# A state-space phase on Trainium2: one activation table for Exp and Ln, decays made early around Silu, and softplus steps moved by a slot

## The chip, the cores and the metric

The kernel runs on one core of a Trainium2 chip. The metric is the device time of one execution in microseconds. The engines that matter are TensorE (PE, with its weight loads PEld), VectorE (DVE), ScalarE (ACT), GpSimd (POOL) and SyncE (SP, whose queue issues the DMAs named here). Each works through its instructions in program order and meets the others by semaphores.

## The reference, cut to what matters

The whole program is a block of four layers in float32 with residuals: a selective state-space layer (SSM) fed by `ctx_1024`, a mixture of experts, a cross-attention and a ternary feed-forward. The change lies in the SSM layer alone:

```python
x = einsum('ed,bld->bel', in_proj_w, ctx)            # 512 channels, 512 steps, 4 batches
u = silu(causal_depthwise_conv(x, conv_w) + conv_b)  # 4 taps
x_dbl = einsum('ke,bel->bkl', x_proj_w, u)           # dt_lo (16), Bm (16), Cm (16)
delta = softplus(dt_proj_w @ dt_lo + dt_proj_b)
A = -exp(A_log)                                      # 512 channels x 16 states
state = state * exp(delta * A) + (delta * u) * B_t   # for each step t
y_t = sum over the 16 states of state * C_t
y = (y + D * u) * silu(layernorm(x_in))
```

## The kernel before

Channels lie on the 128 partitions, so a batch has four chunks `c` of channels, and a chunk has 16 states, taken two at a time. One *slot* is a pair of states of one chunk: `seq` lists 4 batches x 4 chunks x 8 pairs = 128 slots, `q` counts them and `s = q % 32` is the slot within its batch. The recurrence over 512 steps is one scan instruction on DVE (line 511) for two states, 1024 elements long; the first column of `delta` is overwritten with a huge value, so that the second state starts anew.

For slot q these steps are needed:

- `inputs(q)`, line 488 on POOL: dBu = B x (delta u), made two slots ahead in a ring of 3.
- `decays(q)`, line 497 on ACT: two Exp into dA, made one slot ahead, in PSUM, a ring of 2.
- `scan(q)`, lines 511 and 512: the scan on DVE, then the product with C, on POOL for pairs 0, 2 and 4 and on DVE for the others. The result hc is in a ring of 3.
- `sums(q)`, line 517: PE turns hc and adds it up over the states in yT; it is issued at the end of slot q + 1.

Around them the main loop puts other work into the slots, in an order written out by hand. While batch b is scanned, `ahead(b + 1, s)` prepares the next batch: the convolution as products on PE in slots 0 to 15 (`conv`, line 304; its weights come by `load_wcv` from DRAM), Silu of u in slot 17 (`silu_u`), the projection in 18 and 19, and then, for each of the four chunks, softplus in two-slot steps. Softplus is max(p, 0) + ln(1 + exp(-|p|)) with a correction of the rounding of 1 + e: `steps_a` (the product pdt on PE, Abs, Exp and +1 on ACT), `steps_ln` (Ln on ACT), `steps_b` (lines 443, 444 and 446 on DVE, then du on POOL, line 448). `silu_gz` (slot 28) makes the gate's Silu; `gate`, `take_gate` and `result` apply it. `rows` loads B and C as rows broadcast to all partitions, 1 MB each.

Two more jobs ride along for the attention layer: `values` (every other slot, line 470; `take_values` copies pv and stores v), and `Keys` (`task`: a product pk; `evict`: Square and a scaled copy on ACT, and a store; `squares`: sums of squares on PE; `take`: their small eviction). `key_steps` is called twice a slot, with `ends` false near its start and true at its end.

PSUM is full: banks `pa` (pd, pdt, pgz and most of the keys), `pin` (the convolution, and ln for batches after the first), `pv`, `yT`, and two double banks for dA. ACT's functions live in table sets; a function outside the loaded set is preceded by ACT_TABLE_LOAD in the trace.

Of the kernel before, what the change touches and what calls it, by code (L numbers as in the profile page):

```python
# [17 lines left out]
F32 = mybir.dt.float32  # L18
# [11 lines left out]
P = 128  # L30
# [192 lines left out]
        return z  # L223


@with_exitstack
def ssm_phase(ctx, cm, x_all, w, kv, dr):

# [9 lines left out]
    pda = ctx.enter_context(tc.tile_pool(name="a_pda", bufs=2, space=PSUM))  # L238
    KC = CTX // P
    NP = DS // 2  # L240
    R = 64

    def load_x(b):
# [35 lines left out]
    dtT = cp.tile([DR + 1, DM], F32, name="dtT")  # L279
    nc.scalar.dma_start(dtT[0:DR, :], w["dt_proj_wT"])  # L280
    nc.scalar.dma_start(dtT[DR:, :], w["dt_proj_b"])
    nc.scalar.activation(negA, negA, AF.Exp)

    nc.vector.tensor_scalar(negA, negA, -1.0, -1e-27, ALU.mult, ALU.min)
# [52 lines left out]

    def silu_0(c):
        nc.scalar.activation(st[0]["u"][c], st[0]["u"][c], AF.Silu)

# [33 lines left out]
    def silu_u(b):  # L374
        for u in st[b]["u"]:
            nc.scalar.activation(u, u, AF.Silu)

    def stats(b, c):
        sts = small.tile([P, 6], F32, name="st_a")
        nc.vector.bn_stats(sts, x_all[:, b * NC + c, :])  # L380
        nc.vector.bn_aggr(st[b]["mv"][:, c, :], sts)

    def norm(b):
        s = st[b]
        ve = small.tile([P, NC], F32, name="ve_a")
        nc.gpsimd.tensor_scalar(ve, s["mv"][:, :, 1], EPS, None, ALU.add)
        s["rstd"] = small.tile([P, NC], F32, name="rstd_a")
        nc.gpsimd.tensor_tensor(s["rstd"], ve, half, ALU.pow)
        s["nmr"] = small.tile([P, NC], F32, name="nmr")
        nc.gpsimd.tensor_tensor(s["nmr"], s["mv"][:, :, 0], s["rstd"], ALU.mult)  # L390
        nc.gpsimd.tensor_scalar(s["nmr"], s["nmr"], -1.0, None, ALU.mult)

    def silu_gz(b):
        s = st[b]
        for c in range(NC):
            gz = pool[5].tile([P, S], F32, name="gz")
            nc.scalar.activation(gz, x_all[:, b * NC + c, :], AF.Silu, bias=s["nmr"][:, c:c + 1],
                                 scale=s["rstd"][:, c:c + 1])
            s["gz"].append(gz)

    def project(b):
        pd = st[b]["pd"] = ps.tile([R, S], F32, name="pd", tag="pa")
# [14 lines left out]
                t, bc_dram[b, row:row + NG, :].unsqueeze(0).to_broadcast([P, NG, S]))  # L417
            st[b][name].append(t)

    def steps_a(b, c):  # L420

        s = st[b]
        pdt = s["pdt"] = ps.tile([P, S], F32, name="pdt", tag="pa")
        nc.tensor.matmul(pdt, dtT[:, c * P:(c + 1) * P], s["xd"][0:DR + 1, :], start=True,
                         stop=True)
        e, wt = (pool[1].tile([P, S], F32, name=n) for n in ("e", "wt"))
        s["e"], s["wt"] = e, wt
        nc.scalar.activation(e, pdt, AF.Abs)
        nc.scalar.activation(e, e, AF.Exp, scale=-1.0)
        nc.scalar.activation(wt, e, AF.Identity, bias=cm.ones[:, 0:1])  # L430

    def steps_ln(b):

        s = st[b]
        s["ln"] = (pool[5].tile([P, S], F32, name="ln", tag="gz") if b == 0 else
                   ps.tile([P, S], F32, name="ln", tag="pin"))
        nc.scalar.activation(s["ln"], s["wt"], AF.Ln)

    def steps_b(b, c):

        s = st[b]
        e, wt, ln = s["e"], s["wt"], s["ln"]
        nc.vector.scalar_tensor_tensor(e, wt, 1.0, e, ALU.subtract, ALU.subtract)
        nc.vector.tensor_tensor(e, ln, e, ALU.subtract)
        delta = pool[5].tile([P, S], F32, name="delta")
        nc.vector.scalar_tensor_tensor(delta, s["pdt"], 0.0, e, ALU.max, ALU.add)
        du = pool[5].tile([P, S], F32, name="du")
        nc.gpsimd.tensor_tensor(du, delta, s["u"][c], ALU.mult)


        nc.gpsimd.memset(delta[:, 0:1], RESET)
        s["delta"].append(delta)
        s["du"].append(du)


# [32 lines left out]
            nc.gpsimd.tensor_tensor(dBus[q], st[b]["bb"][i // 2][:, j:j + 2, :],  # L488
                                    st[b]["du"][c].unsqueeze(1).to_broadcast([P, 2, S]), ALU.mult)

    def decays(q):
        if q < len(seq):
            b, c, i = seq[q]
            dAs[q] = pda.tile([P, 2, S], F32, name="dA")
            for j in range(2):
                n = 2 * i + j
                nc.scalar.activation(dAs[q][:, j, :], st[b]["delta"][c], AF.Exp,  # L497
                                     scale=negA[:, c, n:n + 1])
# [56 lines left out]
    def ahead(b, s):  # L555

        if s % 4 == 0 and 4 <= s <= 16:
            take_conv(b, s // 4 - 1)
        if s < 16:
            conv(b, s // 4, (s % 4 * 2, s % 4 * 2 + 1))  # L560
        if s in (4, 8):
            load_wcv(b, s // 4 + 1)
        if s == 17:
            silu_u(b)
            for c in range(NC):
                stats(b, c)
            norm(b)
        if s == 18:
            project(b)
        if s == 19:  # L570
            take_project(b)
        if s in (22, 24, 26, 28):
            steps_b(b, (s - 22) // 2)
        if s in (20, 22, 24, 26):
            steps_a(b, (s - 20) // 2)
        if s in (21, 23, 25, 27):
            steps_ln(b)
        if s == 28:
            silu_gz(b)
        if s == 20 and b + 1 < B:  # L580
            start(b + 1)
        if s == 20 and b + 1 == B:
            load_ctx(0, again=True)
        if s in (26, 28, 30, 31):
            rows(b, (26, 28, 30, 31).index(s))

    def key_bank(shape, name):
        return ps.tile(shape, F32, name=name, tag="pin" if name == "pk" and keys.wide else "pa")  # L590

    keys = Keys(cm, w, kv, small, lambda n: pool[1].tile([P, S], F32, name=f"k_{n}",
                                                         tag={"sq": "e", "kT": "wt"}[n]),
# [1 line left out]

    def key_steps(b, s, ends):

        if b > 0 and not ends and s == 0:
            keys.take()
        if b < B - 1:  # L600
            for j, at in enumerate((14, 17, 29) if b == 0 else (3, 6, 11, 14, 17, 29)):
                if not ends and s == at - 3:
                    keys.load(j, j + 1, pool[2], "k_w")
                if not ends and s == at + 3:
                    keys.take()
                if ends and s == at:
                    keys.wide = at > 16
                    keys.task(b + 1, j)
                if ends and s == at + 1:
                    keys.evict()  # L610
                if ends and s == at + 2:
                    keys.squares()
        if b == B - 2 and ends and s in (18, 22):
            h = s - 18
            keys.load(h, h + HG, pool[2], "wcvc")
        if b == B - 1:
            h = s // 2
            if not ends and s % 2:
                keys.take()

            if ends and s == 31:
                keys.squares()
            if ends and s % 2:
                keys.evict()
            if ends and s % 2 == 0:
                if s < 30:
                    keys.squares()
                keys.wide = True
                keys.task(0, h)
                if h in (HG, 2 * HG):  # L630
                    keys.load(h + HG, h + 2 * HG, pool[2], "wcvc")

    def start(b):
        load_ctx(b)
        load_wcv(b, 0)
        load_wcv(b, 1)


    fold(3)
# [25 lines left out]
    for c in range(NC):  # L665
        stats(0, c)
    norm(0)
    steps_a(0, 0)
    steps_ln(0)
    steps_b(0, 0)  # L670
    decays(0)
    inputs(0)
    inputs(1)
    load_wcv(1, 0)
# [1 line left out]
    load_wv(0)  # L676
    for g in range(1, DS // NG):
        rows(0, g)
    SL = NC * NP
    for q, (b, c, i) in enumerate(seq):  # L680
        inputs(q + 2)
        decays(q + 1)
        key_steps(b, q % SL, False)
        if i == 2 and q > 2:
            result(*seq[q - 3][:2])
        scan(q)
        if i == 3:
            direct(b, c)
        if q == 0:
            silu_gz(0)  # L690
        if q % SL == 8 and b + 1 < B:
            load_x(b + 1)
        if q in (4, 6, 13):
            steps_b(0, len(st[0]["du"]))
        if q in (2, 4, 11):
            steps_a(0, len(st[0]["du"]))
        if q in (3, 5, 12):
            steps_ln(0)
        late = 6 if c == NC - 1 or q < NP else 1
        if i == late + 1:  # L700
            take_gate(b, c)
        if b + 1 < B:
            ahead(b + 1, q % SL)
        if i == late:
            gate(b, c)
        if q % 8 == 2 and q + 8 < len(seq):
            load_wv(q // 2 + 4)
        if q % 2:
            values((b + 1) % B, q % SL // 2, wvs[q // 8])
        elif q > 0:  # L710
            take_values(*last)
        last = (b + 1) % B, q % SL // 2
        sums(q - 1)
        key_steps(b, q % SL, True)
    sums(len(seq) - 1)
    take_values(*last)
    keys.take()
    keys.squares()
    keys.take()
    result(B - 1, NC - 1)  # L720
# [1525 lines left out]
```

## Time and profile before

| | us |
|---|---|
| median of 3 runs (lowest, highest) | 2767.82 (2764.25, 2768.01) |
| the profiled execution | 2769.29 |
| its span, first to last instruction | 2767.4 |
| PE busy in the span | 2539.8 |
| DVE busy | 1486.8 |
| ACT busy | 1274.1 |
| POOL busy | 1181.3 |

The SSM phase is the first fifth: its first scan starts at 40.44 us and its last at 579.20 us, and the routing of the experts begins behind it. Its scans of slot 0 start at 40.44, 193.46, 334.44 and 476.75 us for the four batches; those of slot 16 at 115.05, 256.12, 396.77 and 529.33. A stretch of the profile from one of these to the next is half a batch, 16 slots. "Idle before" in a group is the time in which the engine stood in front of its instructions, with what ended it.

### The profile page before, as it was taken

To read this page: it belongs to the slowest core of one execution; us is meant where nothing else is said; L and a number is where in the kernel's file an instruction comes from. 1 tells how busy PE (TensorE), PEld (TensorE's weight loads), DVE (VectorE), ACT (ScalarE), POOL (GpSimd) and SP (SyncE) were. 2 spreads that over 40 slices of the span, in tenths; PEclk is the share of its full clock that TensorE was granted. 3 is DMA by queue.
4 is the path that set the end of the run, shared out by engine and by line. 5 is a ranking of instruction groups with operands and counts; after the bars stand their busy time and mean duration, and the time that the engine had idled before them with its cause. 6 is when DMAs were issued, how large, how long until landed. Compare 5 with 4: busy or idle time off the path is not lost. (4 is left out here: it accounts for less than half of the span.)

```text
span 2767.4 us, 29904 instructions
## 1 busy us (share of the span) xinstructions
PE 2539.8 (92%) x10107; PEld 1436.0 (52%) x10158; DVE 1486.8 (54%) x2546; ACT 1274.1 (46%) x2363; POOL 1181.3 (43%) x1121
## 2 busy tenths in 40 slices
PE   5989897986899999999985989999999999999997
PEld 2545454653456566666663544445555554555543
DVE  5887877966322223333443365545665666544445
ACT  6675757754323322222332443445555554555543
POOL 4888887961333334443433333224431443121212
PEclk8979797987999999999998999999999999999999
DMA  6253535322656656668986344323332443221200
GB/s 243 81 200 102 200 102 188 119 84 80 195 181 209 209 179 220 222 224 306 343 284 209 122 147 131 95 88 126 114 96 80 126 126 99 80 80 51 64 31 19
DMA packets 198352, 405.21 MB, mean 146 GB/s; under 512 B 30372, under 2 KB 71908, under 8 KB 193073
## 3 DMA queue, kind: packets, MB, share of 16 engines
q1 hardware_dynamic: 155566, 249.86, 26.8%
q0 software_dynamic: 40576, 153.19, 17.4%
q8 instruction: 83, 1.36, 0.2%
q14 instruction: 77, 0.62, 0.1%
q10 hardware_dynamic: 2050, 0.18, 0.1%
HBM read 321.22 MB, written 81.92 MB: 146 GB/s over the span
## 5 line engine op out<-in xcount | busy, mean ns | idle before, releaser
L1827 DVE TENSOR_REDUCE mx<-psc 128x1 f32<-128x512 f32 x256 | 176.5, 690 | 452.5 <-PE psc L1824 446.9
L1191 PE MATMUL pg<-xT,wg 128*128 128x284 f32 (+12 forms) x1536 | 399.9, 404 | 14.2 <-ACT h L1202 12.8
L1191 PEld LDWEIGHTS pg<-xT,wg 128*128 128x128 f32 x1536 | 282.6, 194 | 95.1 <-issue 29.7
L1830 ACT ACTIVATE e<-psc,mx 128x512 f32<-128x512 f32 x256 | 176.0, 687 | 320.4 <-DVE mx L1827 320.0
L488 POOL TENSOR_TENSOR dBu<-bb,du 128x1024 f32<-128x1024 f32 x128 | 299.9, 2367 | 26.8 <-DVE dA L511 19.8
L1132 POOL DMA_INDIRECT xg<-xn_dram,tok x168 | 180.7, 1076 | 209.9 <-PE pt L1175 164.7
L1824 PE MATMUL psc<-kT,qT 128*128 128x512 f32 x512 | 264.0, 597 | 1.6 <-ACT qT L1818 1.6
L1851 PE MATMUL po<-eT,v 128*128 128x512 f32 x512 | 235.0, 602 | 10.3 <-ACT eT L1845 10.2
L1790 PE MATMUL pq<-Wq,xnT 128*128 128x512 f32 x512 | 235.0, 603 | 0.7 <-ACT xnT L1749 0.7
L1860 PE MATMUL px<-Wo,oT 128*128 128x512 f32 x512 | 231.5, 595 | 0.0
L511 DVE TENSOR_TENSOR_SCAN dA<-dA,dBu 128x1024 f32<-128x1024 f32 x80 | 183.1, 2289 | 56.9 <-ACT dA L497 46.4
L1801 POOL TENSOR_SCALAR qms<-qms 128x4 f32<-128x4 f32 x64 | 25.5, 398 | 418.1 <-DVE qms L1799 417.2
L1844 PEld LDWEIGHTS pet<-ident,e 128*128 128x128 f32 x1024 | 126.2, 141 | 147.7 <-issue 124.6
L497 ACT ACTIVATE dA<-delta,negA 128x512 f32<-128x512 f32 x256 | 176.5, 692 | 19.0 <-DVE hc L512 12.6
L470 PE MATMUL pv<-Wv,ctxb 128*128 128x512 f32 x256 | 148.1, 709 | 28.7 <-ACT v L476 28.7
L517 PEld LDWEIGHTS yT<-ident,hc 128*128 128x128 f32 x1024 | 130.1, 153 | 83.1 <-issue 57.9
L1851 PEld LDWEIGHTS po<-eT,v 128*128 128x128 f32 x512 | 97.3, 192 | 139.0 <-issue 117.7
L1132 POOL DMA_INDIRECT yg<-y_dram,pos x128 | 128.9, 1007 | 87.5 <-SPq L757 38.5
L1236 DVE COPY yo<-po 128x512 f32<-128x512 f32 x68 | 47.0, 690 | 219.4 <-PE po L1225 219.3
L1844 PE MATMUL pet<-ident,e 128*128 128x128 f32 x1024 | 154.5, 274 | 6.4 <-DVE e L1836 6.4
L517 PE MATMUL yT<-ident,hc 128*128 128x128 f32 x1024 | 145.3, 293 | 11.1 <-POOL hc L512 6.4
L1836 DVE TENSOR_SCALAR e<-e,tot 128x512 f32<-128x512 f32 x256 | 150.5, 588 | 9.1
(352 smaller groups left out, 4384.6 us busy)
## 6 DMA issues: line engine op xcount, KB each, us to landing
y_dram<-yo SPq DMA_DIRECT2D x110, 256.0 KB
bb<-bc_dram SPq DMA_DIRECT2D x16, 1024.0 KB
cb<-bc_dram SPq DMA_DIRECT2D x16, 1024.0 KB
v_dram<-v SPq DMA_DIRECT2D x64, 256.0 KB
k_dram<-k_kT SPq DMA_DIRECT2D x64, 256.0 KB
Wq<-Wq SPq DMA_DIRECT2D x16, 1024.0 KB
kT<-k_dram SPq DMA_DIRECT2D x64, 256.0 KB
rk<-r_dram SPq DMA_DIRECT2D x64, 256.0 KB
```

The costliest lines, as they stand in the source:

```text
L488: nc.gpsimd.tensor_tensor(dBus[q], st[b]["bb"][i // 2][:, j:j + 2, :], st[b]["du"][c].unsqueeze(1).to_broadcast([P, 2, S]), ALU.mult)
L497: nc.scalar.activation(dAs[q][:, j, :], st[b]["delta"][c], AF.Exp, scale=negA[:, c, n:n + 1])
L511: nc.vector.tensor_tensor_scan(*flat, 0.0, ALU.mult, ALU.add)
L517: nc.tensor.matmul(yT[:, lc, :], t[:, lc * P:(lc + 1) * P], cm.ident, is_transpose=True, start=first and lc == 0, stop=last, skip_group_ch ...
L1132: nc.gpsimd.indirect_dma_start(out=t[0:n, :], out_offset=None, in_=table, in_offset=bass.IndirectOffsetOnAxis(ap=index, axis=0))
L1191: nc.tensor.matmul(pg[:, 0:n], s["wg"][:, c, m * P:(m + 1) * P], s["xT"][:, c, 0:n], start=c == 0, stop=c == NC - 1)
L1790: nc.tensor.matmul(pq.rearrange("p h d -> p (h d)"), xnTs[b * NC + i][:, c, :], s["Wq"][:, c, :], start=c == 0, stop=c == NC - 1)
L1824: nc.tensor.matmul(pscore, st[b, g]["qT"][:, h, i * P:(i + 1) * P], ks[n], start=True, stop=True)
L1827: nc.vector.tensor_reduce(mx, pscore, AX.X, ALU.max, negate=True)
L1844: nc.tensor.transpose(pt[:, kc, :], e[:, kc * P:(kc + 1) * P], cm.ident)
L1851: nc.tensor.matmul(po, v[:, kc, :], eT[:, kc, :], start=kc == 0, stop=kc == KB - 1)
L1860: nc.tensor.matmul(px, oTs[j * HG + h][:, i * P:(i + 1) * P], st[b, g]["Wo"][:, h, :], start=h == 0, stop=h == HG - 1)
```

## The change

- `tables` asks for one table set that holds Exp and Ln. It is called before the first Exp and after each group of Silu.
- In slots 16 and 28 the decays of the slot after next are made as well, into an SBUF buffer of the tag `wcvc` instead of PSUM (`early=True`). The two loads of convolution weights that used this tag from slot 20 go to the ends of slots 29 and 31.
- `silu_gz` goes from slot 28 to 29; the layernorm's statistics go from slot 17 to slots 12 to 15, and `norm` to 16.
- The product pdt is a step of its own, `dt`, issued ahead of the slot's values and sums (for chunk 0 at the end of slot 19). A Relu on ACT reads pdt as well and writes the tile that becomes delta, so `steps_b` adds two SBUF tiles and does not read pdt. +1 moves from `steps_a` to `steps_ln`.
- `steps_b` goes from the middle of slots 22, 24, 26, 28 to the end of 21, 23, 25, 27; `step_du` (du on POOL) stays in 22, 24, 26, 28.
- The keys' tasks start a slot earlier, their evictions and takes move within the slots, and their banks are chosen by task.

```diff
+def tables(nc):
+    nc.scalar.preload_act_table_set("natural_log_exp_and_others")
...
     nc.scalar.dma_start(dtT[DR:, :], w["dt_proj_b"])
+    tables(nc)
     nc.scalar.activation(negA, negA, AF.Exp)
...
     def silu_0(c):
         nc.scalar.activation(st[0]["u"][c], st[0]["u"][c], AF.Silu)
+        if c == NC - 1:
+            tables(nc)
...
         for u in st[b]["u"]:
             nc.scalar.activation(u, u, AF.Silu)
+        tables(nc)
...
             s["gz"].append(gz)
+        tables(nc)
...
-    def steps_a(b, c):
+    def dt(b, c):
+        pdt = st[b]["pdt"] = ps.tile([P, S], F32, name="pdt", tag="pa")
+        nc.tensor.matmul(pdt, dtT[:, c * P:(c + 1) * P], st[b]["xd"][0:DR + 1, :], start=True,
+                         stop=True)
+    def steps_a(b):
         s = st[b]
-        pdt = s["pdt"] = ps.tile([P, S], F32, name="pdt", tag="pa")
-        nc.tensor.matmul(pdt, dtT[:, c * P:(c + 1) * P], s["xd"][0:DR + 1, :], start=True,
-                         stop=True)
-        e, wt = (pool[1].tile([P, S], F32, name=n) for n in ("e", "wt"))
-        s["e"], s["wt"] = e, wt
-        nc.scalar.activation(e, pdt, AF.Abs)
-        nc.scalar.activation(e, e, AF.Exp, scale=-1.0)
-        nc.scalar.activation(wt, e, AF.Identity, bias=cm.ones[:, 0:1])
+        pdt = s.pop("pdt")
+        s["e"], s["wt"] = (pool[1].tile([P, S], F32, name=n) for n in ("e", "wt"))
+        s["relu"] = pool[5].tile([P, S], F32, name="delta")
+        nc.scalar.activation(s["e"], pdt, AF.Abs)
+        nc.scalar.activation(s["relu"], pdt, AF.Relu)
+        nc.scalar.activation(s["e"], s["e"], AF.Exp, scale=-1.0)
     def steps_ln(b):
         s = st[b]
+        nc.scalar.activation(s["wt"], s["e"], AF.Identity, bias=cm.ones[:, 0:1])
...
-    def steps_b(b, c):
+    def steps_b(b):
...
-        delta = pool[5].tile([P, S], F32, name="delta")
-        nc.vector.scalar_tensor_tensor(delta, s["pdt"], 0.0, e, ALU.max, ALU.add)
+        delta = s.pop("relu")
+        nc.vector.tensor_tensor(delta, delta, e, ALU.add)
+        s["delta"].append(delta)
+    def step_du(b):
+        s = st[b]
+        c = len(s["du"])
+        delta = s["delta"][c]
         du = pool[5].tile([P, S], F32, name="du")
...
-    def decays(q):
-        if q < len(seq):
+    def decays(q, early=False):
+        if q < len(seq) and q not in dAs:
             b, c, i = seq[q]
-            dAs[q] = pda.tile([P, 2, S], F32, name="dA")
+            dAs[q] = (pool[2].tile([P, 2, S], F32, name="dA", tag="wcvc") if early else
+                      pda.tile([P, 2, S], F32, name="dA"))
...
+        if 12 <= s < 16:
+            stats(b, s - 12)
+        if s == 16:
+            norm(b)
         if s == 17:
             silu_u(b)
-            for c in range(NC):
-                stats(b, c)
-            norm(b)
...
-        if s in (22, 24, 26, 28):
-            steps_b(b, (s - 22) // 2)
-        if s in (20, 22, 24, 26):
-            steps_a(b, (s - 20) // 2)
+        if s in (20, 22, 24, 26):
+            steps_a(b)
+        if s in (21, 23, 25):
+            dt(b, (s - 19) // 2)
+        if s in (22, 24, 26, 28):
+            step_du(b)
         if s in (21, 23, 25, 27):
             steps_ln(b)
-        if s == 28:
+        if s == 29:
             silu_gz(b)
         if s == 20 and b + 1 < B:
-            start(b + 1)
+            load_ctx(b + 1)
...
+    def ahead_ends(b, s):
+        if s in (16, 28):
+            decays((b - 1) * SL + s + 2, early=True)
+        if s in (29, 31) and b + 1 < B:
+            load_wcv(b + 1, (s - 29) // 2)
+        if s == 19:
+            dt(b, 0)
+        if s in (21, 23, 25, 27):
+            steps_b(b)
...
-            for j, at in enumerate((14, 17, 29) if b == 0 else (3, 6, 11, 14, 17, 29)):
+            for j, at in enumerate((13, 17, 29) if b == 0 else (2, 5, 10, 13, 17, 29)):
...
-                if not ends and s == at + 3:
+                if not ends and s == at + 2:
+                    keys.evict()
+                if ends and s == at + 3:
                     keys.take()
                 if ends and s == at:
-                    keys.wide = at > 16
+                    keys.banks = {17: ("pin", "pin"), 29: ("pin", "pa")}.get(at, ("pa", "pa"))
                     keys.task(b + 1, j)
-                if ends and s == at + 1:
-                    keys.evict()
...
-        if b == B - 2 and ends and s in (18, 22):
-            h = s - 18
-            keys.load(h, h + HG, pool[2], "wcvc")
+        if b == B - 2 and ends and s == 18:
+            keys.load(0, HG, pool[2], "wcvc")
...
         sums(q - 1)
+        if q in (1, 3, 10):
+            dt(0, len(st[0]["delta"]) + (q == 3))
+        if q in (3, 5, 12):
+            steps_b(0)
+            step_du(0)
+        if b + 1 < B:
+            ahead_ends(b + 1, q % SL)
         key_steps(b, q % SL, True)
```

In the last batch, where a key head is done in every second slot, `evict` likewise goes from the end of odd slots to the start of even ones, `take` to the end of odd ones (but for slots 9 and 17), and the weights of heads 4 to 7 are loaded at the end of slot 6 instead of slot 22 of the batch before.

More of the change, by code (lines that the diff above doesn't have):

```diff
@@ L240, in ssm_phase @@
     NP = DS // 2
+    SL = NC * NP
     R = 64
@@ L451, in steps_b @@
         nc.gpsimd.memset(delta[:, 0:1], RESET)
-        s["delta"].append(delta)
         s["du"].append(du)
@@ L585, in ahead @@
             rows(b, (26, 28, 30, 31).index(s))
+    def ahead_ends(b, s):
[7 more added lines that the diff above has]
+            steps_b(b)
     def key_bank(shape, name):
-        return ps.tile(shape, F32, name=name, tag="pin" if name == "pk" and keys.wide else "pa")
+        return ps.tile(shape, F32, name=name, tag=keys.banks[name == "kpss"])
     keys = Keys(cm, w, kv, small, lambda n: pool[1].tile([P, S], F32, name=f"k_{n}",
@@ L596, in key_steps @@
     def key_steps(b, s, ends):
-        if b > 0 and not ends and s == 0:
+        if b > 0 and ends and s == 0:
             keys.take()
         if b < B - 1:
-            for j, at in enumerate((14, 17, 29) if b == 0 else (3, 6, 11, 14, 17, 29)):
-                if not ends and s == at - 3:
+            for j, at in enumerate((13, 17, 29) if b == 0 else (2, 5, 10, 13, 17, 29)):
+                if not ends and s == max(at - 3, 0):
                     keys.load(j, j + 1, pool[2], "k_w")
-                if not ends and s == at + 3:
+                if not ends and s == at + 2:
+                    keys.evict()
+                if ends and s == at + 3:
                     keys.take()
                 if ends and s == at:
-                    keys.wide = at > 16
+                    keys.banks = {17: ("pin", "pin"), 29: ("pin", "pa")}.get(at, ("pa", "pa"))
                     keys.task(b + 1, j)
-                if ends and s == at + 1:
-                    keys.evict()
                 if ends and s == at + 2:
                     keys.squares()
-        if b == B - 2 and ends and s in (18, 22):
-            h = s - 18
-            keys.load(h, h + HG, pool[2], "wcvc")
+        if b == B - 2 and ends and s == 18:
+            keys.load(0, HG, pool[2], "wcvc")
         if b == B - 1:
             h = s // 2
-            if not ends and s % 2:
+            if s % 2 and ends == (s not in (9, 17)):
                 keys.take()
-            if ends and s == 31:
+            if s == 31 and ends:
                 keys.squares()
-            if ends and s % 2:
+            if s % 2 == 0 and not ends:
                 keys.evict()
-            if ends and s % 2 == 0:
+            if s % 2 == 0 and ends:
                 if s < 30:
                     keys.squares()
-                keys.wide = True
+                keys.banks = "pin", "pa"
                 keys.task(0, h)
[L630 to L636, printed above, removed]
+                if h in (HG - 1, HG, 2 * HG):
+                    h = max(h + HG, 2 * HG - 1) // HG * HG
+                    keys.load(h, h + HG, pool[2], "wcvc")
     fold(3)
@@ L667, in ssm_phase @@
     norm(0)
-    steps_a(0, 0)
+    dt(0, 0)
+    steps_a(0)
     steps_ln(0)
-    steps_b(0, 0)
+    steps_b(0)
+    step_du(0)
     decays(0)
+    decays(1)
     inputs(0)
@@ L678, in ssm_phase @@
         rows(0, g)
-    SL = NC * NP
     for q, (b, c, i) in enumerate(seq):
@@ L692, in ssm_phase @@
             load_x(b + 1)
-        if q in (4, 6, 13):
-            steps_b(0, len(st[0]["du"]))
         if q in (2, 4, 11):
-            steps_a(0, len(st[0]["du"]))
+            steps_a(0)
         if q in (3, 5, 12):
@@ L713, in ssm_phase @@
         sums(q - 1)
+        if q in (1, 3, 10):
+            dt(0, len(st[0]["delta"]) + (q == 3))
+        if q in (3, 5, 12):
+            steps_b(0)
+            step_du(0)
+        if b + 1 < B:
+            ahead_ends(b + 1, q % SL)
         key_steps(b, q % SL, True)
@@ L717, in ssm_phase @@
     keys.take()
+    keys.evict()
     keys.squares()
```

## The prediction

> **What bounds the kernel now.** I went from the time slices (VectorE and GpSimd are busiest up to about 580 us, which is the state-space phase that the diff touches) to the busy times by stretch, cut at the scans of line 511 that begin a half of a batch's 32 slots. Columns: stretch, length, busy us of PE, PEld, DVE, ACT, POOL, PE clock, DMA share, GB/s.
>
> ```profile
> 193.46:256.12 62.66, 62.66 (x278) 37.63 (x277) 49.44 (x29) 33.94 (x58) 54.87 (x25) 1.00 0.43 140
> 256.12:334.44 78.32, 63.35 (x231) 35.46 (x230) 61.02 (x50) 63.15 (x90) 60.52 (x36) 0.78 0.45 156
> 476.75:529.33 52.58, 50.84 (x272) 34.01 (x271) 48.80 (x29) 38.05 (x69) 51.34 (x24) 1.00 0.43 147
> ```
>
> The first row is slots 0 to 15 of batch 1: PE busy all of it at full clock, so PE sets the time. The second is slots 16 to 31: 15.7 us longer, and no engine is full. The third, batch 3, prepares no next batch: POOL (51.3 of 52.6) sets it. Batch 2 repeats batch 1 (62.3 and 80.0), batch 0's second half takes 78.4. So three halves of about 78 us are open. Next, what the scan waited for in the second stretch, and ACT's groups there:
>
> ```profile
> its engine sat idle before it (us, times) until:
>   ACT dA L497: 13.9, 9
>   PE yT L517: 1.6, 1
>   POOL dBu L488: 1.2, 1
> ```
>
> ```profile
> L497 ACT ACT_TABLE_LOAD x6 | 7.7, 1283 | 0.1
> L437 ACT ACT_TABLE_LOAD x4 | 5.1, 1283 | 0.1
> L428 ACT ACTIVATE e<-pdt 128x512 f32<-128x512 f32 x4 | 2.4, 597 | 6.5 <-PE pdt L424 6.5
> L376 ACT ACT_TABLE_LOAD x1 | 1.3, 1283 | 0.0
> L397 ACT ACT_TABLE_LOAD x1 | 1.3, 1283 | 0.0
> ```
>
> DVE waits 13.9 us for decays, and ACT has 12 table loads and stands 6.5 us at Abs, whose product (L424) needs the bank that line 446 on DVE frees. The largest single hole, from the timeline of ACT and the waits of that stretch:
>
> ```profile
> 319.84 1.28 ACT L397 ACT_TABLE_LOAD   x1
> 321.13 2.93 ACT L397 ACTIVATE gz<-x_all,nmr,rstd_a 128x512 f32<-128x512 f32 x4
> 323.97 0.56 ACT L476 COPY v<-pv 128x512 f32<-128x512 f32 x1
> 324.55 1.28 ACT L497 ACT_TABLE_LOAD   x1
> 325.84 2.75 ACT L497 ACTIVATE dA<-delta,negA 128x512 f32<-128x512 f32 x4
> ```
>
> ```profile
> PE pv L470 <- ACT v L476: 8.8, 5, 5.3
> ```
>
> Silu with its two loads holds the decays (scan 30 waits 3.8) and the copy of v (PE waits 5.3 at 319.3, and then carries that backlog into the PE-bound half).
>
> **Part 1, tables.** Of 12 loads a half, 4 stay (two around each Silu): 8 x 1.30 = 10.4 us of ACT. Before slot 16 of batch 0, the head included, 8 more go. Relu adds four; not in the trace, taken as Abs (0.60): 2.4. Net 8 us of ACT, which counts only where DVE waits. The row: decays end at 283.96, load at 283.97, Ln at 285.27, so 1.30. The Trainium skill ("ScalarE: Activation LUTs", What ACT_TABLE_LOAD costs) adds a drain of some 1.38 and says 2.66 a switch: 21.3 a half, which would promise the whole 13.9. The trace has no drain; I keep 1.30.
>
> **Part 2, operands that move to SBUF.** Line 446 took max(pdt) from PSUM; now it adds relu and e, both SBUF. Slots 18 and 30 get their dA in SBUF, beside dBu and cb. DVE and POOL in batch 0, where ln too is in SBUF (two timelines):
>
> ```profile
> 62.11 0.82 DVE L443 SCALAR_TENSOR_TENSOR e<-wt,e 128x512 f32<-128x512 f32 x1
> 63.03 2.65 DVE L444 TENSOR_TENSOR e<-ln,e 128x512 f32<-128x512 f32 x1
> 65.72 0.69 DVE L446 SCALAR_TENSOR_TENSOR delta<-pdt,e 128x512 f32<-128x512 f32 x1
> ```
>
> ```profile
> 60.03 5.10 POOL L488 TENSOR_TENSOR dBu<-bb,du 128x1024 f32<-128x1024 f32 x2
> 65.11 2.79 POOL L512 TENSOR_TENSOR hc<-hc,cb 128x1024 f32<-128x1024 f32 x1
> ```
>
> Line 444 took 2.65 instead of 0.69: it ended 0.55 after POOL's product did (65.14), and POOL's next took 2.79 instead of 2.36. Line 446, with a PSUM operand, took 0.69 beside POOL. The Trainium skill ("SBUF — State Buffer", SBUF: two separate sides) has the rule: a DVE operation with two SBUF inputs and a GpSimd operation that reads SBUF exclude each other for a whole instruction. It speaks against this change: four additions, two scans and one product a half newly need the lock. For the scan no row shows it: unlocked it is 2.29, at worst it waits a whole POOL product (2.3) and holds POOL 2.2. I take the lock. Without it this sum would be about 7 us a half better.
>
> **Part 3, the half again by hand** (batch 1, t = 0 at 256.12; a POOL product each 2.31 us, 2.2 after a lock; a DVE operation 0.55 after one).
> Scan 19: ACT does conv's Identity, v, dA 18, k_ms, load, four Silu (2.45), load, dA 19: 13.8, before 14.1. The stats (3.4 us of DVE), now in slots 12 to 15 where DVE waits for PE, hid beside that chain. Norm (1.9 us of POOL) goes ahead of dBu 19. Scan 18 waits for POOL (8.5 to 10.5), inside the same wait.
> Scan 20 needs the sums of 17, behind project, whose bank waits for gzT behind dA 19: 18.9, before 19.4. Scan 21: 21.2, before 21.6.
> Slot 21 now ends with lines 443, 444 and the addition. Mult 21 ends 24.8; wt comes 27.2 and Ln 27.8 (Abs at 22.5 behind dt, then Relu, Exp, v, dA 22). POOL's dBu 23 runs to 27.7, then dBu 24 in front of the addition to 30.5. Scan 22: 31.1; scan 23: 34.6, before 33.6.
> Scans 25, 27, 29: 43.5, 53.4, 63.1; before 43.7, 53.3, 63.8. ACT's stalls are gone, but 443 waits 1.1, 0.1 and 0.6 and the addition 0, 1.4 and 1.4.
> Silu of gz hides beside slots 29 and 30. Scan 30 waits 0.1, its product 2.1 for dBu 31. Scan 31: 72.3, before 74.8; scan 32: 75.8, before 78.3.
> Gain 2.5 a half, 7.5 in three.
>
> **Part 4, PE's backlog.** v is copied ahead of Silu, so the 5.3 us wait goes. The sums of 32 come at 82.3 instead of 86.7, held by POOL's hc 32 (81.4): 4.4, of which 2.5 is counted. The rest, 1.9, counts in batches 1 and 2, where PE is full: 3.8. Keys one slot earlier only reorder PE: by the sums of 15 the work is the same.
>
> **Part 5, taken as nothing.** The head: softplus is 2 us shorter, but dBu 2 waited for bb to 48.48. Batch 0's three early steps save loads and pay a third lock (ln in SBUF): 0, from -2 to +3. du on POOL keeps its slot, behind the same dBu. Evict goes behind the decays: its store on SP goes 1.4 later, with the v store behind it; two slots of 3.3 us cover that; k_ms taken at a slot's end only has to free its bank before the next product, a slot later; without that cover PE waits those 1.4 us for each of 12 keys in batches 1 and 2, 17 us. wcvc for the next batch: from slot 20 to ends of 29 and 31 on SP, behind 2 and 4 MB of rows. Around there DMA moved 270 to 400 GB/s, so a load and the rows in front are 7 us; the first is wanted 10 us later, the second in slot 4, 12 us later. If late, PE stands still one for one. Wk for heads 4 to 7: 512 KB, two slots (6.7 us) ahead. POOL enters batch 3, where it is the bound, with more backlog: +1, and the last keys +0.3.
>
> **Sum.** 7.5 + 3.8 - 1.3 = 10. The profiled execution took 2769.3 (span 2767.4, 1.9 around it), 1.5 over the median 2767.8. 10 off the median: 2758.
>
> **Rivals.**
> A, forecast: locks eat most: 2758 (2746 to 2766). For: the 2.65 us row. Chance 0.42.
> B, locks miss: the new operations fall into POOL's waits (it is busy 60.5 of 78.3). 7 a half more: 2758 - 21 = 2737. Against: once ACT is quick, POOL's holes close. 0.26.
> C, nothing: the half is worth 0 to 1 because PE's project, sums 17 and POOL pace it anyway, and PE's full halves don't shift: 2766. 0.16.
> D, slower: DVE now reaches 443 in the slot of its Ln, and Ln stands behind decays that wait for DVE's own product. By hand Ln is done 0.7 us before that product in slots 23 and 25, and level with it in 27. If ACT is later, DVE idles in 12 pairs and every scan behind waits: from 0.8 us a pair the gain is gone (12 x 0.8), at 1.5 it is +18: 2776. For: slot 21 does it already. Against: ACT has 8 us less to do. 0.12.
> E, the loads don't go: if Exp still asks for its own set, the four tables() a stage add loads (4 x 1.3, in three batches 16): 2780. 0.04.
>
> **Numbers.** A measurement of this kernel tells about 0.2%, 5.5 us, from no change. Of A, 0.35 lies faster by that and 0.07 within; with B faster is 0.61, with C same 0.23, D and E slower 0.16. The range goes from below B to D: 2733 to 2776. A alone is 2746 to 2766.
>
> **What would show it.** Right: four ACT_TABLE_LOAD in a second half, none at Ln; the wait of scan for ACT dA under 3 us; the addition that replaces 446 at 0.55 to 2.2 with a mean over 1.2; PE pv no longer waiting 5 us for v; the second half 74 to 77 us. B: the addition's mean at 0.7 and halves of 69. D: line 443 idle on ACT wt or ln in most pairs. E: loads in front of Exp. Wrong altogether: PE waiting for DMA wcvc in slots 0 to 4, or first halves longer than 63 us.

## The result, and the profile after

The changed kernel took 2758.36 us (median of 7 runs, 2754.28 to 2760.97) against 2768.01 before (7 runs beside them, 2764.25 to 2776.38): ratio 0.9959, interval 0.9944 to 0.9974. So it is faster by 0.41%, more than the 0.2% that counts as a difference. The forecast was 2758 (2733 to 2776); rival A, in which locks eat most of the gain, came in.

The profiled execution took 2754.28 (span 2752.6) against 2769.29. Of these 15.0 us, 10.9 lie in the state-space phase: its last scan starts at 568.26 instead of 579.20. The rest is code that, but for the last key, the change does not touch, and its length wanders between 2184.2 and 2193.1 over all 14 profiles of this study. So the fit of the total to 0.4 us is partly luck. The phase is the better ruler, and even there scan 2 of batch 0, which waits for a row's DMA, starts at 50.3 to 52.4 in one execution or another. From here on I compare the phase net of it, from scan 2 to the last scan: 528.3 before, 515.9 after, 12.5 less.

The busy times by stretch, cut as in the prediction where the scan of slot 0 or 16 begins (stretch, length, busy us of PE, PEld, DVE, ACT, POOL, PE clock, DMA share, GB/s):

```profile
191.49:254.28 62.79, 62.79 (x269) 36.89 (x269) 52.16 (x38) 36.58 (x61) 56.98 (x26) 1.00 0.43 143
254.28:328.35 74.07, 59.61 (x241) 35.59 (x240) 64.92 (x41) 51.56 (x82) 64.11 (x35) 0.82 0.45 162
464.80:518.36 53.56, 49.62 (x257) 32.45 (x258) 48.80 (x29) 36.20 (x66) 53.56 (x25) 1.00 0.45 141
```

PE still fills the first half of batch 1. The second half is 4.25 shorter (78.32 before), and ACT is busy 11.6 less in it. The first half of batch 3 is 1.0 longer, with POOL busy all of it. What the scan waited for in the second row's stretch, and ACT's groups there:

```profile
its engine sat idle before it (us, times) until:
  PE yT L540: 3.6, 2
  ACT dA L520: 2.7, 1
```

```profile
L228 ACT ACT_TABLE_LOAD x2 | 2.6, 1283 | 0.0
L443 ACT ACTIVATE e<-pdt 128x512 f32<-128x512 f32 x4 | 2.4, 598 | 9.6 <-DVE delta L462 6.0 <-PE kpss L1152 3.7
L385 ACT ACT_TABLE_LOAD x1 | 1.3, 1283 | 0.0
L407 ACT ACT_TABLE_LOAD x1 | 1.3, 1283 | 0.0
```

The wait for decays fell from 13.9 to 2.7, and 12 loads became four, none at Ln. But ACT's stall at Abs did not go. It grew from 6.5 to 9.6, of which 6.0 is now the wait for DVE's addition (line 462) to release `e`. The other 3.7 are a key's: its Square goes into the same buffer, and the sums kpss read it. After Silu of gz, ACT's timeline shows the second load, the decays, and the copy of v behind them:

```profile
315.34 1.51 ACT L407 ACTIVATE gz<-x_all,nmr,rstd_a 128x512 f32<-128x512 f32 x2
316.86 1.28 ACT L228 ACT_TABLE_LOAD   x1
318.16 1.42 ACT L520 ACTIVATE dA<-delta,negA 128x512 f32<-128x512 f32 x2
319.51 0.58 ACT L497 COPY v<-pv 128x512 f32<-128x512 f32 x1
```

PE no longer waits 5 us for v: in this half no wait of its matmuls for v is left. The lock (DVE and POOL shutting each other out, part 2 of the prediction), in slot 21, DVE's rows and then POOL's:

```profile
279.76 1.16 DVE L459 SCALAR_TENSOR_TENSOR e<-wt,e 128x512 f32<-128x512 f32 x1 [2.67 <-ACT wt L450]
281.02 0.69 DVE L460 TENSOR_TENSOR e<-ln,e 128x512 f32<-128x512 f32 x1
281.75 1.93 DVE L462 TENSOR_TENSOR delta<-delta,e 128x512 f32<-128x512 f32 x1
283.61 2.29 DVE L534 TENSOR_TENSOR_SCAN dA<-dA,dBu 128x1024 f32<-128x1024 f32 x1
```

```profile
278.01 5.11 POOL L509 TENSOR_TENSOR dBu<-bb,du 128x1024 f32<-128x1024 f32 x2
```

Line 460, whose ln lies in PSUM, takes 0.69. Line 462, with both inputs in SBUF, takes 1.93 and ends 0.56 after POOL's product (283.12). DVE also stands 2.67 at line 459, waiting for wt.

**Where the stretches are cut.** The half before slot 16 did not become shorter (62.66 and 62.79), though the prediction wanted 1.9 there. The saving is one scan later: before, the scan of slot 17 (260.31) began 4.19 after that of slot 16, having waited 1.90 for decays that stood on ACT behind a key's Square and copy, and the Square had waited 2.45 for PE:

```profile
257.74 0.60 ACT L1100 ACTIVATE k_sq<-pk 128x512 f32<-128x512 f32 x1 [2.45 <-PE pk L1091]
258.80 1.42 ACT L497 ACTIVATE dA<-delta,negA 128x512 f32<-128x512 f32 x2
```

After, it begins 2.21 later, but the scan of slot 16 waits 1.91 for PE yT. It is PE's work on either side of the cut. So I cut the tables below at the scans of slots 1 and 17.

| us between scans | 2 to 17 | 17-33 | 33-49 | 49-65 | 65-81 | 81-97 | 97-127 | 2 to 127 |
|---|---|---|---|---|---|---|---|---|
| before | 68.4 | 76.4 | 64.7 | 76.3 | 64.3 | 78.0 | 100.2 | 528.3 |
| after | 67.5 | 73.8 | 62.8 | 74.1 | 62.6 | 73.8 | 101.3 | 515.9 |

Batch 1's second half in this cut (scans 49 to 65), before and after:

```profile
260.31:336.63 76.32, 61.35 (x236) 35.49 (x235) 60.91 (x49) 62.55 (x90) 59.89 (x36) 0.78 0.48 168
256.48:330.55 74.07, 59.61 (x244) 35.84 (x243) 64.92 (x43) 52.95 (x86) 66.31 (x36) 0.82 0.47 171
```

DVE's wait for decays is 11 us shorter, but it is idle only 6.3 less, since other waits take part of the place, and it is busy 4.0 more, although 3.4 us of statistics have left this half. That leaves 2.3 of gain.

The first column, scans 2 to 17, also wanders from one execution to the next. Two kernels of this study whose code is the same up to scan 17, the run with the sum in PSUM (first row) and the changed kernel:

```profile
51.01:120.07 69.06, 64.10 (x240) 36.00 (x241) 58.23 (x42) 37.54 (x62) 56.32 (x29) 0.90 0.38 134
52.38:119.91 67.53, 62.10 (x246) 35.20 (x246) 60.91 (x42) 37.47 (x62) 57.26 (x29) 0.95 0.38 135
```

They differ by 1.5 us, at granted clocks of 0.90 and 0.95. So the surer ruler runs from scan 17 to the last: 460.0 before, 448.3 after, 11.6 less. Each kernel has one profile, so differences of a few tenths mean nothing.

### The profile page after: what moved, and what is told of

The parts are those of the page before. It is cut to its first block, busy times and chain, and to the rows that moved or that the text cites. A ratio compares the mean times of both kernels' runs of the same rounds, so it can differ in the third digit from the quotient of the medians.

```text
span 2752.6 us, 29943 instructions
## 1 busy us (share of the span) xinstructions
PE 2526.8 (92%) x10158; PEld 1428.8 (52%) x10158; DVE 1512.0 (55%) x2546; ACT 1236.7 (45%) x2347; POOL 1196.8 (43%) x1121
## 5 line engine op out<-in xcount | busy, mean ns | idle before, releaser
L1232 PE MATMUL pg<-xT,wg 128*128 128x284 f32 (+12 forms) x1536 | 398.9, 404 | 16.8 <-ACT h L1243 15.2
L509 POOL TENSOR_TENSOR dBu<-bb,du 128x1024 f32<-128x1024 f32 x128 | 318.2, 2509 | 22.1 <-DVE dA L534 13.6
L1173 POOL DMA_INDIRECT wd<-down,widx x64 | 62.0, 969 | 221.5 <-PE po L1266 202.2
```

The source lines that it names most:

```text
L1173: nc.gpsimd.indirect_dma_start(out=t[0:n, :], out_offset=None, in_=table, in_offset=bass.IndirectOffsetOnAxis(ap=index, axis=0))
L1232: nc.tensor.matmul(pg[:, 0:n], s["wg"][:, c, m * P:(m + 1) * P], s["xT"][:, c, 0:n], start=c == 0, stop=c == NC - 1)
```

## Experiments

Theory: ACT's waits go, by the table loads and by the new order, and locks give part of that back. Rivals: the loads were hidden, and where the steps stand makes the time; or the locks cost nothing. "Last scan" is where the scan of the last pair starts; "net" is from scan 2, "from 17" from scan 17. In short:

| kernel | last scan | net | from 17 | median us | ratio to before (interval) |
|---|---|---|---|---|---|
| before | 579.20 | 528.3 | 460.0 | 2768.01 | 1 |
| before, tables alone | 578.03 | 526.8 | 456.9 | 2767.22 | 0.9983 (0.9973, 0.9992) |
| before, dt ahead and Relu alone | 582.03 | 530.4 | 460.6 | 2768.63 | 0.9990 (0.9983, 0.9998) |
| after | 568.26 | 515.9 | 448.3 | 2758.36 | 0.9959 (0.9944, 0.9974) |
| after, no tables | 568.12 | 516.1 | 448.3 | 2759.17 | 0.9960 (0.9944, 0.9977) |
| after, sum in PSUM | 562.08 | 511.1 | 442.0 | 2753.40 | 0.9921 (0.9904, 0.9937) |
| after, no early decays | 566.48 | 516.0 | 448.5 | 2756.86 | 0.9942 (0.9925, 0.9958) |
| after, steps_b in slots 22 to 28 | 563.80 | 512.1 | 444.6 | 2755.07 | 0.9925 (0.9906, 0.9945) |
| after, Silu of gz in slot 28 | 570.39 | 519.2 | 451.6 | 2759.57 | 0.9963 (0.9947, 0.998) |
| after, batch 0's steps a slot later | 567.67 | 517.3 | 448.2 | 2761.28 | 0.9967 (0.9952, 0.9982) |
| after, stats in slot 17 | 569.02 | 517.8 | 452.7 | 2758.96 | 0.9950 (0.9935, 0.9965) |
| after, keys in their old slots | 567.82 | 516.2 | 448.7 | 2758.36 | 0.9953 (0.9935, 0.9971) |
| the three lock and place edits together | 555.84 | 505.5 | 438.0 | 2747.08 | 0.9918 (0.990, 0.9937) |
| the same, no tables | 558.70 | 506.9 | 439.4 | 2751.97 | 0.9927 (0.991, 0.9944) |

Many intervals of the changed versions overlap; those are told apart by the phase, not by the medians.

### The table set alone, on the kernel before

```diff
+def tables(nc):
+    nc.scalar.preload_act_table_set("natural_log_exp_and_others")
...
             nc.scalar.activation(u, u, AF.Silu)
+        tables(nc)
...
```

> The kernel before with the table set alone; order, decays and steps stay. Marks: the last scan starts at 579.20 us before and at 568.26 us after. Theory (loads count only where a scan waits behind them): decays of slots 25, 29 and 30 stand behind removed loads, those of 22, 24 and 26 stand behind the bank that line 446 frees; of 13.9 us of waits for dA a half, 3 to 4 go, so the last scan comes at 568 to 571 and the time is 8 to 11 us lower. Rival (the loads are the waits): 10.4 us a half go, last scan at 548, 31 us lower. Rival (loads were hidden): 579, no change. [...]

The loads went and the time hardly moved: 1.5 us net, 3.0 from scan 17, a median 0.17% lower (0.08 to 0.27). Of the second halves, those of batches 0 and 2 are 1.8 and 2.9 shorter and that of batch 1 is 1.0 longer (77.3). ACT's group of Abs in batch 1's shows where the saved time went:

```profile
L438 ACT ACTIVATE e<-pdt 128x512 f32<-128x512 f32 x4 | 2.4, 599 | 16.5 <-PE pdt L434 16.5
```

The wait at Abs went from 6.5 to 16.5: the eight loads' 10.4 us turned into waiting for a bank that DVE frees a slot later, and the scans still waited 13.0 for decays (13.9 before). My theory, that the set alone was worth 8 to 11 us, fell.

### dt ahead and Relu alone, on the kernel before

```diff
+        s["relu"] = pool[5].tile([P, S], F32, name="delta")
         nc.scalar.activation(e, pdt, AF.Abs)
+        nc.scalar.activation(s["relu"], pdt, AF.Relu)
...
-        nc.vector.scalar_tensor_tensor(delta, s["pdt"], 0.0, e, ALU.max, ALU.add)
+        delta = s.pop("relu")
+        nc.vector.tensor_tensor(delta, delta, e, ALU.add)
...
+        if s in (21, 23, 25):
+            dt(b, (s - 19) // 2)
...
```

> The kernel before with one part of the change: the product pdt of chunks 1 to 3 is issued in slots 21, 23 and 25, and a Relu frees its bank, so that Abs no longer waits for line 446; the sum is then the addition of two SBUF tiles, with its lock. Loads, slots of the steps, Silu, statistics and keys stay as before. Measure: from scan 17 to scan 17 + 16 of batches 0, 1, 2: before 76.4, 76.3, 78.0; after 73.8, 74.1, 73.8. Theory (the loop delta, bank, pdt, Abs, decays set the second halves, not the loads): 2 us a pair less, 1 to 4 us a half back to the lock: 72 to 75, last scan at 568 to 575. Rival (it takes the loads away as well): no change, 579.

Missed: no gain. The phase is 2.1 longer net, but 1.4 of that lie before scan 17, where two executions of the same code differed by as much; from scan 17 it is 0.6 longer, and the median of 20 runs is 0.1% lower. So it is not shown to be slower, and it is no faster to speak of. The bank no longer holds Abs up, but the next link of the same chain does (ACT's group, and the addition's row, ns min/median/max):

```profile
L435 ACT ACTIVATE e<-pdt 128x512 f32<-128x512 f32 x4 | 2.4, 598 | 5.6 <-DVE delta L454 4.4 <-PE pdt L423 1.2
```

```profile
L454 DVE TENSOR_TENSOR delta<-delta,e x4: 692/1928/1936, 291.8 to 321.2; 128x512 f32<-128x512 f32 x4
```

Abs waits 4.4 for `e`, and the addition itself takes 1.93 in place of 0.69. What the scan waited for in batch 1's second half:

```profile
  ACT dA L505: 7.5, 6
  POOL dBu L496: 4.2, 2
```

The wait for decays does fall, from 13.9 to 7.5; the wait for POOL's dBu (1.2 before) and the longer additions take it back.

### The changed kernel without the table set

```diff
-    nc.scalar.preload_act_table_set("natural_log_exp_and_others")
+    pass
```

> The kernel after without the shared table set: Exp and Ln load their own sets again, 8 more loads a half; everything else as after. The set alone moved nothing in the order before (last scan 578.03 instead of 579.20). Theory (with the loop through the bank of pdt cut, ACT's loads come to stand in front of Ln and dA, which DVE now needs in the same slot): 1.5 to 2.6 us a pair, last scan at 580 to 595, slower than before. Rival (loads are hidden in the new order too, and the moved steps alone are the gain): 568 to 570.

The phase has 49 loads again instead of 17, which is 42 us of ACT, and the last scan moved 0.1 us. ACT's groups in batch 1's second half:

```profile
L520 ACT ACT_TABLE_LOAD x6 | 7.7, 1283 | 0.1
L453 ACT ACT_TABLE_LOAD x4 | 5.1, 1283 | 0.1
L443 ACT ACTIVATE e<-pdt 128x512 f32<-128x512 f32 x4 | 2.4, 593 | 4.0 <-PE kpss L1152 3.7 <-DVE delta L462 0.3
```

The 6.0 of waiting for the addition is 0.3: the loads fill the time in which ACT would stand there. What the scan waited for in the same half:

```profile
  PE yT L540: 3.6, 2
  ACT dA L520: 2.7, 1
```

That is the list of the changed kernel to the tenth. So the wait for decays went from 13.9 to 2.7 by the other parts of the change, not by the loads. From both sides, then, the table set by itself is worth little: 3.0 from scan 17 in the old order, nothing in the new one. My theory fell again, and the rival held.

### The sum in PSUM

```diff
-        nc.vector.tensor_tensor(e, ln, e, ALU.subtract)
+        e2 = e if b == 0 else ln
+        nc.vector.tensor_tensor(e2, ln, e, ALU.subtract)
         delta = s.pop("relu")
-        nc.vector.tensor_tensor(delta, delta, e, ALU.add)
+        nc.vector.tensor_tensor(delta, delta, e2, ALU.add)
```

> The kernel after, but line 460 writes its result into ln's PSUM bank (batches 1 to 3), so that the addition of relu has one SBUF operand. Lock theory: the addition takes 0.69 in every pair (after: 0.69 to 1.95), POOL's dBu beside it is not held, and 2 to 3 us a half go: last scan at 560 to 563 (after 568.26), 5 to 8 us below the kernel after. Rival (POOL sets the pace, the lock's wait is slack): 567 to 568, the same time as after.

Line 460 writes where ln lies (in batch 0, where ln is in SBUF, all stays), so the addition has one input in PSUM. The addition's row, after and then with this edit:

```profile
L462 DVE TENSOR_TENSOR delta<-delta,e x16: 691/1920/1954, 34.6 to 448.2; 128x512 f32<-128x512 f32 x16
```

```profile
L463 DVE TENSOR_TENSOR delta<-delta,ln x12: 686/686/689, 145.3 to 441.2; 128x512 f32<-128x512 f32 x12
```

Not one of 12 additions waits, where the median was 1.92. The phase is 4.8 shorter net and 6.3 from scan 17; the code before scan 17 is the same, so 6.3 is the edit's: 2.1, 2.3 and 1.9 in the three second halves, as the lock theory had it. The same edit stops the addition from reading `e`, so ACT gets it back earlier, and the two are not separated here. That ACT's wait for `e` does not cost much by itself is seen below, with steps_b in its old slots.

### No early decays

```diff
-        if s in (16, 28):
-            decays((b - 1) * SL + s + 2, early=True)
```

> The kernel after without the early decays: the dA of slots 18 and 30 are made in their usual place, in PSUM. Theory (the early decays pay by the lock about what they save on ACT): scans 18 and 30 and the product of 30 run unlocked, dBu beside them takes 2.35 instead of 4.3; Silu of gz starts later, behind dA 30, which waits for scan 28; 0 to 1 us a half better, last scan at 565 to 568 (after 568.26). Rival (the early decays carry Silu): scans 19 and 31 wait 2 to 4 us more, last scan at 574 to 580.

Net 0.1: the decays made ahead bought what the lock on scans 18 and 30 cost, and no more. The lock itself is gone, as expected: dBu beside these scans takes 2.36 or 2.37 in all three batches, where the changed kernel had 4.17 to 4.43 in five of the six places. Beside scan 18 of batch 1:

```profile
258.78 2.37 POOL L509 TENSOR_TENSOR dBu<-bb,du 128x1024 f32<-128x1024 f32 x1
```

### steps_b back in slots 22, 24, 26, 28

```diff
         if s in (22, 24, 26, 28):
+            steps_b(b)
...
-        if s in (21, 23, 25, 27):
-            steps_b(b)
```

> The kernel after, but the three DVE lines of softplus stand where they stood before, in slots 22, 24, 26 and 28 (batches 1 to 3), in front of the next chunk's Abs. Theory (moving them a slot earlier costs the wait for wt in slot 21 and returns it as an earlier delta that nobody needs): line 459 no longer idles 2.7 us, scan 22 starts 4 us earlier, scan 23 1 us earlier; 0 to 2 us a half better, last scan at 562 to 568 (after 568.26). Rival (the earlier place is what lets ACT's Abs go early, since e has one buffer): the wait of Abs returns with 2 us a pair, last scan at 575 or later. Rival (the wait in slot 21 is a net loss): 2.7 us a half, 560.

The phase is 3.8 shorter, so the earlier slot was a cost. DVE's stall of 2.67 at line 459 is gone (no wait is listed under its row), and the row is quicker too, with a median of 0.96 where the changed kernel had 1.23 in this half:

```profile
L459 DVE SCALAR_TENSOR_TENSOR e<-wt,e x4: 680/957/1725, 281.0 to 309.2; 128x512 f32<-128x512 f32 x4
```

ACT, meanwhile, stands longer at Abs than in the changed kernel, 15.2 instead of 9.6:

```profile
L443 ACT ACTIVATE e<-pdt 128x512 f32<-128x512 f32 x4 | 2.4, 597 | 15.2 <-DVE delta L462 11.6 <-PE kpss L1152 3.7
```

The rival that this wait sets the pace fell: ACT has this time to spare.

### Silu of gz back in slot 28

```diff
-        if s == 29:
+        if s == 28:
             silu_gz(b)
```

> The kernel after with the Silu of gz back in slot 28, ahead of that slot's copy of v and of dA 30. Theory (part 4 of the prediction: the copy of v behind Silu makes PE carry a backlog into the next half, which PE sets): PE's wait for v of about 5 us returns at the end of each half, scan 30 waits 2 to 4 us, and the first halves of batches 1 and 2 start 1 to 2 us later on PE; last scan at 574 to 580 (after 568.26). Rival (Silu's place costs nothing once dA 30 is early): 568 to 570.

Net 3.3 slower: the last scan came at 570.39, where 574 to 580 was forecast. The largest wait of PE in batch 1's second half is back (waiter, who it waited for, us, times, longest):

```profile
PE pv L491 <- ACT v L497: 6.1, 1, 6.1
```

Batch 1 pays in both halves (49 to 65: 76.3, and 33 to 49: 64.0). Batch 2's full half stays 62.6, although these 6.1 us lie just ahead of it, so the backlog that I expected to pass into it shows once, not twice.

### Three smaller undos

Batch 0's three steps a slot later:

```diff
+        if q in (4, 6, 13):
+            steps_b(0)
+            step_du(0)
...
-        if q in (3, 5, 12):
-            steps_b(0)
-            step_du(0)
```

> The kernel after with batch 0's three early softplus steps (DVE lines and du) at their old place, slots 4, 6 and 13 in front of the next Abs. In batch 0 ln is in SBUF, so the lines need the lock three times. Scan 17 starts at 119.23 before and 119.91 after, though scan 1 starts 1.2 earlier. Theory (the earlier place makes DVE wait for Ln and the lock ahead of scans 4, 6 and 13): scan 17 at 117 to 118.5. Rival (PE sets batch 0's first half, or the lock costs the same anywhere): 119.5 to 120.5.

My theory (scan 17 at 117 to 118.5) fell: it came at 119.4. Scans 2 to 17 took 69.1 instead of 67.5, but the sum-in-PSUM run, with the steps in the earlier place, took 69.1 as well. So which place is better is not shown; from scan 17 on the two kernels are alike. That batch 0 came later to scan 17 after the change (119.9, before 119.2) was the row's DMA in the head: from scan 2 it is 0.8 quicker.

Stats and norm back in slot 17:

```diff
-        if 12 <= s < 16:
-            stats(b, s - 12)
-        if s == 16:
-            norm(b)
         if s == 17:
             silu_u(b)
+            for c in range(NC):
+                stats(b, c)
+            norm(b)
```

> The kernel after with the layernorm statistics and norm back in slot 17. Theory (3.4 us of DVE hide beside ACT's Silu chain, which ends at scan 19 either way): scan 17 to 33 stays at 73.8 to 75, last scan at 568 to 571. Rival (they stand in front of result and so of PE's sums of 16, project and sums of 17): 2 to 3.4 us a half, last scan at 574 to 578.

Net 1.9 slower, and the last scan (569.02) is where I expected it, but for another reason. The second halves are 2.2, 1.2 and 1.1 longer (76.0, 75.2, 74.9; the theory's limit was 75), so there the move is worth 4.4 from scan 17. Scans 2 to 17 took 65.1 instead of 67.5: in batch 0 the move costs 2.4. Scans 13 to 17, with the stats in slot 17 and then as changed:

```profile
103.50:116.30 12.80, 12.80 (x52) 7.13 (x51) 12.49 (x9) 6.42 (x11) 10.68 (x6) 1.00 0.11 41
104.66:119.91 15.25, 14.79 (x68) 8.88 (x66) 14.83 (x14) 7.25 (x12) 10.74 (x6) 1.00 0.09 34
```

DVE is nearly full there (12.49 of 12.80), so the statistics lengthen these slots; in batch 1, where PE is full, scans 33 to 49 take 62.8 either way.

The keys of batches 0 to 2 in their old slots:

```diff
-            for j, at in enumerate((13, 17, 29) if b == 0 else (2, 5, 10, 13, 17, 29)):
+            for j, at in enumerate((14, 17, 29) if b == 0 else (3, 6, 11, 14, 17, 29)):
...
```

> The kernel after with the key steps of batches 0 to 2 in their slots of before (tasks a slot later, Square and copy ahead of the next slot's decays, takes at a slot's start). Measure: from scan 33 to 49 and 65 to 81, which PE sets: before 64.6 and 64.3, after 62.8 and 62.6. Theory as predicted (keys only reorder PE; the first halves gain by PE's missing backlog): still 62.6 to 62.8. Rival (with Silu of gz back, one of these halves stayed at 62.6, so the gain is the keys' order): 64.3 to 64.8, last scan at 571 to 573.

Net 0.3. The full halves of batches 1 and 2 are 63.4, between the two forecasts (after: 62.8 and 62.6), and the halves after them are 0.5 shorter: the keys move work over the cut. In these two batches the scan of slot 17 again starts 3.83 after that of slot 16 (4.19 before the change).

### Sum in PSUM, no early decays and steps_b in slot 22 together

The three edits above in one kernel, the best version of the study.

> The kernel after with three edits at once: the addition reads its second operand from PSUM (alone: last scan 562.08), no early decays (alone: 566.48), and the three DVE lines in slots 22, 24, 26 and 28 (alone: 563.80); after is at 568.26. Theory (three separate prices): they add up to 12.4, last scan at 555 to 558, about 12 us under after. Rival (they take away the same wait, POOL or PE paces below it): last scan at 560 to 562, no better than the best of them.

The phase is 10.4 shorter net than after the change (12.4 by the last scan), and the median of 2747.08 (2745.51 to 2749.22) beats both kernels. Batch 0's and batch 1's second halves, cut at slots 1 and 17:

```profile
117.82:185.34 67.52, 51.73 (x211) 29.08 (x210) 59.79 (x42) 51.89 (x83) 61.84 (x36) 0.89 0.50 175
250.23:321.40 71.17, 55.45 (x239) 31.85 (x238) 59.91 (x43) 52.65 (x86) 61.86 (x36) 0.90 0.47 165
```

POOL is busy 61.8 of 67.5 and 61.9 of 71.2, where the changed kernel had 66.3 of 74.1 in batch 1: the products that stood in the lock are shorter. The three prices add up: from scan 17 the edits alone gave 6.3, -0.1 and 3.7, which makes 9.9, and together they gave 10.3.

### The same without the table set

> The kernel of e7 (no new locks, last scan 555.84) without the shared table set, as e6 was the kernel after without it (568.12 against 568.26: no change). Theory (in the kernel after, DVE waits for POOL's lock longer than for the loads, which hide them; without the locks DVE comes to wait for dA 25, 27 and 29 behind Ln's two loads): about 1 us a pair, 3 to 4 us a half, last scan at 563 to 570. Rival (the shared set is worth nothing in any of these orders): last scan at 555 to 558.

The loads were to show once the locks are gone, with 3 to 4 us a half; that was a miss. The phase is 1.4 us longer net, from one profile each, and the intervals of the two ratios overlap. So the kernel without a table set is 21.5 us net ahead of before, and the set adds 1.4 at most.

## Why the prediction was right, and where it was not

**Part 1, tables.** Counts and price held: four loads a half, 1.30 each. The Trainium skill ("ScalarE: Activation LUTs", What ACT_TABLE_LOAD costs) would put a drain of some 1.38 beside each; after the change Silu ends at 316.85, the load starts at 316.86 and Exp at 318.16, so again none. The step that failed is "Net 8 us of ACT, which counts only where DVE waits": I let it count in the half's sum, and it does not. Over all batches the loads are worth 1.5 us net in the kernel before (3.0 from scan 17), 0.3 after and 1.4 in the best order, because ACT stands waiting in that time without them.

**Part 2, the lock.** Right in kind, too dear by a factor of two. The addition's median is 1.92 (forecast: mean over 1.2), and with a PSUM operand it falls to 0.69. The scan, for which no row of before spoke, takes the lock too: beside scan 18 (first row), whose dA is now in SBUF, POOL's first dBu took 4.28 of the 6.58 that the two products of the second row took, and DVE's product of slot 30 (third row) took 3.12 instead of 1.23.

```profile
260.81 2.31 DVE L534 TENSOR_TENSOR_SCAN hc<-dA,dBu 128x1024 f32<-128x1024 f32 x1
```

```profile
260.99 6.58 POOL L509 TENSOR_TENSOR dBu<-bb,du 128x1024 f32<-128x1024 f32 x2
```

```profile
321.78 3.12 DVE L535 TENSOR_TENSOR hc<-dA,cb 128x1024 f32<-128x1024 f32 x1
```

The sum put the lock of all this at about 7 us a half against its absence. Taking out the addition's lock, the early decays and the earlier slot gave 10.3 from scan 17, 3.4 a half, and that includes the wait for wt. The kernel without them took 2747, not the 2737 that the 7 a half stood for.

**Part 3, the half by hand.** With one offset (252.3, slot 17 standing at 4.19 as before) the scans of slots 19, 21, 23, 25, 27, 29, 31 and 32 were due at 266.1, 273.5, 286.9, 295.8, 305.7, 315.4, 324.6 and 328.1. They came at 265.83, 273.46, 287.14, 296.05, 305.81, 315.53, 324.82 and 328.35. In slot 21 the course held as well: line 459 was to wait 2.4 for wt and waited 2.67. In slots 23, 25 and 27 it was to wait 1.1, 0.1 and 0.6, and no wait is listed. Nor does the timetable rest on part 1: without the table set the three second halves are 73.8, 74.1 and 74.0. They were to gain 2.5 each and gained 2.6, 2.3 and 4.2. The excess is in batch 2, whose half was the longer before (78.0, with 15.5 of waits for decays); after, all three are alike. The sum had taken them as equal; no run isolated why that one was longer. That the statistics would hide in slots 12 to 15 held in batches 1 and 2, where PE is full, but not in batch 0, where they cost 2.4.

**Part 4, PE's backlog.** The size held, 1.9 in each full half (measured 1.9 and 1.7 by the cut at slots 17 and 1). The cause is shown for batch 1 alone: with gz in slot 28 the wait for v and 1.2 of that full half returned, but batch 2's full half stayed at 62.6 behind a wait of 6.1, so what shortened it is open. "Keys one slot earlier only reorder" held (0.3 net).

**Part 5, taken as nothing.** Batch 3 lost the 1.0 put down for it (it came back without the early decays, and with steps_b in slots 22 to 28). PE waited for no DMA of `wcvc`. Batch 0's earlier steps, put at 0, show no difference beyond what executions of the same code differ by. Moving the stats gained 1.9 in all.

**Rivals.** B fell with the addition's median, C with 11.6 us from scan 17, E with 17 loads in the phase (its own term, 16 us on 2758, would make 2774, not 2780). D named a real place: line 459 waits 2.67 for wt once in batch 1's half, and putting the steps a slot earlier cost 3.8 in all. It did not reach its deciding point of 0.8 us in each of 12 pairs (9.6).

**What stays open.** From scan 17 no single undo loses more than 4.4 of the 11.6 (the statistics; the Silu of gz 3.3), and the tables, the early decays and the keys move it by less than 0.4. dt and Relu were never taken out of the changed kernel: alone on the kernel before they bring nothing, and whether the rest of the gain needs them was not tried. On the kernel before, that pair took the wait for decays from 13.9 to 7.5; what took it on to 2.7 is known only as far as that it was not the loads. The table set together with dt and Relu on the kernel before was not tried either.

## What to carry to other kernels

Before counting on an engine's saved time, ask what it would wait for next: here 42 us of ScalarE went or came and the phase moved by 0.1 to 3 us, because ScalarE then stood waiting for a single buffer that VectorE frees. Nor is a long wait of an engine a cost as such: with steps_b in its old slots ScalarE stood 15.2 us at Abs instead of 9.6, and the phase was 3.8 shorter. When an operand moves from PSUM to SBUF, look at what GpSimd is doing at that moment; an addition of 0.69 us became 1.92, and writing the intermediate into the PSUM bank where its operand ln lay took it back. A long change is worth undoing piece by piece: two of its parts, the early decays and the earlier slot, brought nothing or cost time, and without them and the lock the kernel is faster still. And a ruler has to be tested on code that did not change: here the same code differed by 1.5 us between two profiles.

## What the runs showed of the hardware that was not expected

VectorE's scan with both inputs in SBUF shuts GpSimd's product out for its whole length, as an elementwise operation does: the dBu beside scan 18 took 4.28 us, and 2.37 in the run where the scan's dA lay in PSUM. The Trainium skill ("SBUF — State Buffer", SBUF: two separate sides) gives the rule for VectorE and GpSimd operations; these rows show it for the scan. In two rows the waiting VectorE operation went ahead of GpSimd's next one: the addition of slot 21 ended 0.56 us after GpSimd's product, as line 444 had (0.55) in the row of before.
